# Rescheduling a two-layer bottleneck kernel: first stages further ahead, positions later, filters by halves

## The chip, the cores and the metric

One core of a Trainium2 chip runs the kernel. The engines of a core work side by side, each from its own queue of instructions in order: PE (TensorE: matrix products and transposes), DVE (VectorE), ACT (ScalarE), POOL (GpSimd, which here issues the gathers) and SP (SyncE, which here issues most other transfers). The metric is device time in microseconds (us) for one execution of the whole program; a time quoted as a median is over several executions.

## What is computed

The input x is (4, 1024, 56, 56), float32, and passes through two bottleneck layers.

Layer 0 is a deformable bottleneck. `_conv` is a convolution with bias:

```python
r = jax.nn.relu(_conv(x, w1, b1))                                  # 1x1, 1024 -> 256
r = jax.nn.relu(_deform_conv3x3(r, w2, b2, w_off, b_off))           # 3x3, 256 -> 256
r = _conv(r, w3, b3)                                               # 1x1, 256 -> 1024
x = jax.nn.relu(x + r)
```

In the deformable 3x3 convolution a plain 3x3 convolution of r (256 to 18 channels) gives two offsets for each pixel and each of the nine taps. Each tap reads r at the pixel's place, plus the tap's step, plus its offset, interpolated bilinearly between four neighbours. The nine results are multiplied by the tap's 256 x 256 weights and summed.

Layer 1 is a plain bottleneck with batch normalisation over all four images after each convolution:

```python
out = jax.nn.relu(_bn(_conv(x, w1, b1, 1, 0), g1, be1))             # 1x1, 1024 -> 256
out = jax.nn.relu(_bn(_conv(out, w2, b2, 1, 1), g2, be2))           # 3x3, 256 -> 256
out = _bn(_conv(out, w3, b3, 1, 0), g3, be3)                        # 1x1, 256 -> 1024
x = jax.nn.relu(x + jax.nn.softplus(residual_scale)[0] * out)
```

## The kernel before, in words

**Blocks and stages.** Each image n (four of them) is worked in seven blocks j. Layer 0 passes through these stages; each stage is a Python generator that yields the cost of the matmuls that it has just issued.

- The first stage, `stage_a` (L312 to L427), handles eight rows (448 pixels) of an image. It multiplies x by w1 (matmul L326 over eight chunks of channels, added to a bias that L283 puts into PSUM) and clips the result into `feat` (L318, on ACT). `for_offsets` (L402) multiplies `feat` by the offset weights (`pm`, L407), copies the result (`part`, L416) and stores it in `offc` by small DMAs (L424). `to_table` (L371) transposes `feat` on PE (`ftp`, L380), copies it to the tile `ft` on ACT (L387, L389, L390), and stores it from there in a DRAM table (L394, L398) from which the taps gather. While its own products run, a first stage loads the x of the next block, `following` (`load_x`, L260 to L275, issued on SP). Image 0's seven first stages come ahead of all taps and use a variant of the products with fewer multiplications (class `First`).
- The positions, `stage_b` (L433 to L483): PE transposes a part of `offc` (`po`, L443), ACT copies it (`off`, L458), and about twenty small DVE operations (L459 to L481) turn offsets into gather indices (`idxs`) and bilinear weights (`wts`) for one tap block. In `stage_a(n, j)` the positions of block j - 2 are worked (`if j > 1`), and those of the last two blocks by `last_positions(n)` (L681).
- The taps. The 3136 pixels of an image are cut into tap blocks of 512, 512, 512, 512, 384, 384 and 320 (`SIZES`), and each has nine taps k, 252 in all. `sample` (L489) issues one gather on POOL for each 128 pixels (L495; four neighbours x 256 channels), scales the first neighbour on ACT (L505), and adds the other three on DVE (L507, three instructions). `turn` (L517) transposes the samples on PE (`stp`, L532), copies them on ACT (L538, into `sts`), and forms three sums on DVE (L540 to L542). `tap` (L548) makes the seven products of a Strassen-Winograd step (L560). After tap 8, ACT copies the sums out (L575 to L579), DVE combines them into `r2` (L581 to L587), and ACT clips them (`r`, L589).
- The last stage, `stage_c` (L594 to L667), for one tap block: for each of eight chunks of 128 channels, ACT copies the residual x into PSUM (`pr`, L612), PE adds the product with w3 (L616), ACT clips (`x1t`, L627), and SP stores. The residual is loaded by L605. Then layer 1's 1x1 convolution is done on the same pixels (`acc`, L642), with a copy (L652), statistics (L656) and a store (L657).

**After the taps** layer 1 goes on: a Winograd 3x3 convolution with the transformed filters that `filters` (L685 to L740) made on the way, in the taps of image 3, from loads (L698) and eleven DVE operations on 128 x 1536 elements (L702 to L721), then the statistics, the last 1x1 convolution and the output.

**What sets the order.** The main loop (L944 to L1030) goes through the 252 taps. At tap i it issues the turn of tap i + 1, the samples of tap i + 2 and the products of tap i. Then it adds to a budget the tap's share of all other matmul work (`share`, worked out so that first and last stages come out even over all taps), and steps generators until the budget is spent. `next_stage` (L959) chooses the generator: a first stage of the next image if it is at most one block ahead of the tap block (`first_ones[0][1] <= j + 1`, L961) and in step with the part of the image that has passed, or if no last stage is waiting; otherwise a last stage of a finished tap block from `last_ones`. If there is neither, the loop breaks and the budget stays for later. `due` forces the first stages of the next image to be finished near the image's end. `waiting` holds `last_positions(n)` and is served at once, out of the budget, from the first tap of an image on.

The program order isn't quite the order on the chip: a scheduler under the kernel orders the instructions into the engines' queues, with waits between engines where one needs another's result.

**Buffers.** `gat` has eight gather tiles, `w3p` eight sample tiles `s` and two `sts`, `xin` four tiles for x of first stages, `work` five tiles `r2`, and `worka` one `ft`.

## Time and profile before

| what | value |
|---|---|
| median of three executions | 2836.54 us (2831.96 to 2837.84) |
| the profiled execution | 2833.8 us |
| its span, first to last instruction | 2832.0 us |
| mean granted clock of PE in it | 0.986 |
| matmuls on PE (x12045): busy | 2739.8 us, 97% of the span |
| DVE (x5188): busy | 2175.3 us, 77% |
| ACT (x3045): busy | 1500.8 us, 53% |
| POOL (x1054): busy | 1217.2 us, 43% |
| bytes moved by DMA | 792.70 MB, mean 280 GB/s |
| first tap products, image 0 / 1 / 2 / 3 | 152.5 / 645.7 / 1117.3 / 1597.1 us |
| last tap block's end of products | 2077.3 us |

How to read it: the profile is of one execution. Each engine's busy time is what its instructions took, and since the engines overlap, the shares don't add up to one. An instruction's line (L616) is the line of the kernel that issued it; `pr<-r,w` names what it writes and reads. In a timeline, the number in brackets is how long the engine was idle before the instruction, and what released it. PE can be granted a lower clock after it has been idle; the clock row and the clock columns show that in tenths and as a fraction.

### The profile page before, as it was taken

What the parts mean: (1) busy time and instruction counts of PE and PEld (TensorE: products, weight loads), DVE (VectorE), ACT (ScalarE), POOL (GpSimd) and SP (SyncE); (2) the same over time, 40 slices, a digit from 0 to 9 for tenths busy, and PEclk for the clock granted to TensorE, in tenths of its full rate; (3) what the DMA queues carried; (4) which work ended last, traced back from release to release, by engine and by line L of the source; (5) the groups of instructions that cost most, each with busy time, mean ns of one, the idle gap of its engine ahead of it and who ended that gap; (6) DMA issues with size and microseconds to landing.
All of it is one profiled execution on the core that took longest, in us unless ns stands there. A gap on an engine that the chain in (4) does not pass through costs nothing.

```text
span 2832.0 us, 39691 instructions
## 1 busy us (share of the span) xinstructions
PE 2739.8 (97%) x12045; PEld 1932.4 (68%) x12045; DVE 2175.3 (77%) x5188; ACT 1500.8 (53%) x3045; POOL 1217.2 (43%) x1054
## 2 busy tenths in 40 slices
PE   9979999999999999999999989999989999999999
PEld 7655566677766676667666657666769999874554
DVE  5387777888787889778878888878849987437777
ACT  2245555665655556555564656666652554514444
POOL 0065666576666455656545666554500000111211
PEclk9989999999999999999999999999999999999999
DMA  8598998999999999999998989999930110219998
GB/s 287 180 342 322 327 318 296 362 323 343 342 347 358 337 313 333 338 339 343 359 343 261 349 310 342 350 375 323 314 130 24 48 36 12 93 34 345 352 342 304
DMA packets 313319, 792.70 MB, mean 280 GB/s; under 512 B 33769, under 2 KB 134673, under 8 KB 313105
## 3 DMA queue, kind: packets, MB, share of 16 engines
q0 software_dynamic: 127296, 462.48, 46.0%
q1 hardware_dynamic: 167376, 276.30, 28.4%
q10 hardware_dynamic: 18432, 51.39, 4.6%
q8 instruction: 95, 1.56, 0.2%
q14 instruction: 120, 0.97, 0.1%
HBM read 640.94 MB, written 143.75 MB: 277 GB/s over the span
## 4 chain that ended last, share of the span: by engine, by line
PE 81%; DMA 8%; DVE 6%; ACT 3%; issue 1%; SPq 1%; POOL 0%; ACTq 0%; DVEq 0%; POOLq 0%
PE acc L560 19%; PE acc L642 11%; PE pr L616 10%; PE acc L326 9%; PE q L1192 6%; PE stp L532 6%; DMA g<-table,idxs 5%; PE u L1642 4%; PE c L1642 3%; PE v L1642 3%; PE acc_g L1474 2%; PE pm L407 2%; DVE s L507 2%; PE b L1192 2%; DMA xr<-in_x_dram 1%
## 5 line engine op out<-in xcount | busy, mean ns | idle before, releaser
L495 POOL DMA_INDIRECT g<-table,idxs x900 | 1143.5, 1271 | 908.9 <-DVE s L507 264.2
L507 DVE SCALAR_TENSOR_TENSOR s<-g,wts,s 128x256 f32<-128x256 f32 (+1 forms) x2700 | 1171.9, 478 | 309.7 <-ACT s L505 301.4
L560 PE MATMUL acc<-sts,w 128*128 128x256 f32 (+2 forms) x3528 | 729.0, 356 | 3.7 <-ACT sts L538 2.4
L560 PEld LDWEIGHTS acc<-sts,w 128*128 128x128 f32 x3528 | 604.4, 191 | 54.8 <-ACT sts L538 5.0
L505 ACT ACTIVATE s<-g,wts 128x256 f32<-128x256 f32 x900 | 427.2, 511 | 292.5 <-DMA g<-table,idxs 150.7
L616 PE MATMUL pr<-r,w 128*128 128x512 f32 (+2 forms) x896 | 372.2, 553 | 22.3 <-ACT pr L612 17.1
L642 PE MATMUL acc<-x1t,c1w 128*128 128x512 f32 (+2 forms) x896 | 357.6, 541 | 3.4 <-ACT acc L283 2.2
L532 PEld LDWEIGHTS stp<-ident,s 128*128 128x128 f32 (+1 forms) x1800 | 212.0, 141 | 139.6 <-issue 84.6
L326 PE MATMUL acc<-xt,w 128*128 128x448 f32 x704 | 282.1, 545 | 6.6 <-DMA xt<-in_x_dram 6.6
L616 PEld LDWEIGHTS pr<-r,w 128*128 128x128 f32 x896 | 166.8, 194 | 160.1 <-issue 83.3
L532 PE MATMUL stp<-ident,s 128*128 128x128 f32 (+1 forms) x1800 | 254.8, 274 | 18.1 <-DVE s L507 13.0
L642 PEld LDWEIGHTS acc<-x1t,c1w 128*128 128x128 f32 x896 | 167.9, 190 | 145.1 <-issue 92.6
L538 ACT COPY sts<-stp 128x512 f32<-128x512 f32 (+2 forms) x504 | 242.1, 529 | 19.8 <-PE stp L532 19.7
L627 ACT ACTIVATE x1t<-pr,ch 128x512 f32<-128x512 f32 (+2 forms) x224 | 141.6, 632 | 133.1 <-PE pr L616 130.4
L326 PEld LDWEIGHTS acc<-xt,w 128*128 128x128 f32 x704 | 132.9, 192 | 113.9 <-issue 111.2
L1593 ACT ACTIVATE x1f<-x1f,sh_bn 128x896 f32<-128x896 f32 x112 | 116.0, 1041 | 150.7 <-DVE x1f L1590 125.5
L652 ACT COPY y<-acc 128x512 f32<-128x512 f32 (+2 forms) x112 | 59.2, 529 | 193.2 <-PE acc L642 193.1
L542 DVE TENSOR_TENSOR sts<-sts 128x512 f32<-128x512 f32 (+2 forms) x252 | 155.5, 617 | 0.7
L612 ACT COPY pr<-xr 128x512 f32<-128x512 f32 (+2 forms) x224 | 121.3, 542 | 4.6 <-DMA xr<-in_x_dram 0.3
L1590 DVE SCALAR_TENSOR_TENSOR x1f<-u,sc_bn,x1f 128x448 f32<-128x448 f32 x156 | 106.6, 684 | 18.8 <-PE u L1642 9.4
L1192 PE MATMUL q<-v,u 128*128 128x196 f32 x576 | 108.4, 335 | 8.5 <-DVE v L1144 7.7
L540 DVE TENSOR_TENSOR sts<-sts 128x256 f32<-128x256 f32 (+2 forms) x252 | 97.1, 385 | 24.7 <-ACT sts L538 24.0
(302 smaller groups left out, 3054.0 us busy)
## 6 DMA issues: line engine op xcount, KB each, us to landing
xt<-in_x_dram SPq DMA_DIRECT2D x112, 448.0 KB
x1f<-x_d SPq DMA_DIRECT2D x96, 448.0 KB
out_dram<-x1f ACTq DMA_DIRECT2D x96, 448.0 KB
xr<-in_x_dram SPq DMA_DIRECT2D x128, 256.0 KB
x_d<-x1t SPq DMA_DIRECT2D x128, 256.0 KB
table<-ft SPq DMA_DIRECT2D x56, 384.0 KB
g<-table,idxs POOLq DMA_INDIRECT x900, 7.4
xr<-in_x_dram SPq DMA_DIRECT2D x64, 192.0 KB
```

What stands on the lines that cost most here:

```text
L326: nc.tensor.matmul(acc, w1[:, k, h * 128 : (h + 1) * 128], xts[n, j, k - k % 2][:, k % 2, :], start=start, stop=(k == KC - 1), skip_group_ ...
L495: nc.gpsimd.indirect_dma_start(out=g[:m], out_offset=None, in_=tables[n].rearrange("r q c -> r (q c)"), in_offset=bass.IndirectOffsetOnAxi ...
L505: nc.scalar.activation(s[:m], g[:m, 0:CB], AF.Copy, scale=wt[:, 0])
L507: nc.vector.scalar_tensor_tensor(s[:m], g[:m, corner * CB : (corner + 1) * CB], wt[:, corner], s[:m], ALU.mult, ALU.add,)
L532: nc.tensor.transpose(banks[h][:, t * 128 : t * 128 + m], s[:m, h * 128 : (h + 1) * 128], ident[:m, :m],)
L538: nc.scalar.copy(to, banks[h][:, :size].rearrange("p (e q) -> p e q", e=2))
L542: nc.vector.tensor_sub(sts[:, 5:7, :half], sts[:, 1:4:2, :half], sts[:, 0:2, :half])
L560: nc.tensor.matmul(sums[i], w2[:, a, k], sts[:, b, :half], start=(k == 0 and i % 2 == 0), stop=(k == TAPS - 1), skip_group_check=True,)
L616: nc.tensor.matmul(z, w3[:, h, k * 128 : (k + 1) * 128], r2[:, h, :size], start=False, stop=(h == KB - 1), skip_group_check=True,)
L642: nc.tensor.matmul(z, c1w[:, k, h * 128 : (h + 1) * 128], x1ts[k], start=False, stop=(i == KC // 2 - 1), skip_group_check=True,)
L1192: nc.tensor.matmul(ps[:, o].rearrange("p r c -> p (r c)"), wt, x, start=first and j == 0 and (alone or o == 0), stop=last and j == len(pai ...
L1642: nc.tensor.matmul(to, wt, x, start=start, stop=stop, skip_group_check=True)
```

## The change

Five things are changed together.

- Positions: in images 1 to 3 a first stage works the positions of the block four behind, and no longer two behind (`positions_behind`). `last_positions` therefore has four blocks left, and one step of it is made at each even tap k while any is left, outside the loop that spends the budget. Each step finishes one block's positions (copy and DVE operations) and issues the transposes of the next, so four blocks take five steps, at taps 0, 2, 4, 6 and 8 of tap block 0.
- First stages may run three blocks ahead of the tap block instead of one. With that go two changes of buffers: x of block (1, 2) is loaded by the first stage of (1, 0), and that of (1, 1) loads nothing; and `ft` of block (0, 6) lies in a gather tile instead of `worka`'s only one.
- The clip of a tap block's results (L589) becomes `clip_taps`, called one tap later, just before the block joins `last_ones`.
- The filters' eleven operations are made by halves of 768 columns, and the generator is stepped at eight of nine taps instead of at four.
- `share` leaves out half a block more of last-stage work, which so stays for after the taps (`SIZES[-1] * 3 // 2` instead of `SIZES[-1]`).

```diff
@@ -309,6 +309,11 @@
 
 
 
+        def positions_behind(n):
+
+
+            return 2 if n == 0 else 4
+
         def stage_a(n, j):
 
             b = n * NJ + j
@@ -333,6 +338,9 @@
                 )
 
             following = (n, j + 1) if j + 1 < NJ else (n + 1, 0)
+            if n == 1 and j < 2:
+
+                following = (1, 2) if j == 0 else (N, 0)
             if (n, j) == (0, 0):
 
                 sums = [
@@ -358,18 +366,24 @@
                     for k in range(KC):
                         product(h, k, z, False)
                         if k % 2:
-                            if h == KB - 1 and following != (1, 1):
+                            if h == KB - 1:
                                 load_x(*following, k - 1)
                             yield 2 * BLK
                     clip(h, z, 0.0)
 
                 yield from run([channels(h) for h in range(KB)])
-            if j > 1:
-                yield from stage_b(n, j - 2)
+            behind = positions_behind(n)
+            if j >= behind:
+                yield from stage_b(n, j - behind)
             yield None
 
             def to_table():
-                ft = worka.tile([128, QFULL + 1, CB], F32, tag="ft", name=f"ft_{b}")
+                if (n, j) == (0, NJ - 1):
+
+                    ft = gat.tile([128, 4 * CB], F32, tag="g", name=f"ft_{b}")
+                    ft = ft.rearrange("p (t c) -> p t c", c=CB)
+                else:
+                    ft = worka.tile([128, QFULL + 1, CB], F32, tag="ft", name=f"ft_{b}")
                 for half in range(2):
                     tp = ps1.tile([128, 2, CB], F32, tag="bank", name=f"ftp_{b}_{half}")
                     for i in range(2):
@@ -585,11 +599,17 @@
                 add(r[0][1], r[0][1], p3)
                 add(r[1][0], r[1][1], p4)
                 add(r[1][1], r[1][1], p5)
-                for o in range(KB):
-                    nc.scalar.activation(
-                        r2[:, o, :size], r2[:, o, :size], AF.Relu, bias=col("a_b2", o)
-                    )
                 r2s[n, j] = r2
+
+        def clip_taps(n, j):
+
+            size = SIZES[j]
+            r2 = r2s[n, j]
+            for o in range(KB):
+                nc.scalar.activation(
+                    r2[:, o, :size], r2[:, o, :size], AF.Relu, bias=col("a_b2", o)
+                )
+            last_ones.append((n, j))
 
         def stage_c(n, j):
 
@@ -679,7 +699,7 @@
             nc.scalar.activation(mv[:, 0, 0:1], eps_t, AF.Sqrt)
 
         def last_positions(n):
-            for j in (NJ - 2, NJ - 1):
+            for j in range(NJ - positions_behind(n), NJ):
                 yield from stage_b(n, j)
 
         def filters():
@@ -697,28 +717,37 @@
             for i, t in ((0, w_0), (2, w_2), (1, u3)):
                 nc.sync.dma_start(t.rearrange("p (h j o) -> p h j o", h=KB, j=3), rows[i])
             yield
-            stt = nc.vector.scalar_tensor_tensor
-
-            nc.vector.tensor_add(u1, w_0, w_2)
-            yield
-            nc.vector.tensor_sub(u2, u3, u1)
-            yield
-            nc.vector.tensor_add(u1, u3, u1)
-            yield
-            nc.vector.tensor_scalar_mul(u2, u2, 1.0 / 6)
-            nc.vector.tensor_scalar_mul(u1, u1, -1.0 / 6)
-            yield
-
-            stt(u4, w_2, 4.0, w_0, ALU.mult, ALU.add)
-            yield
-            stt(u3, u3, 2.0, u4, ALU.mult, ALU.add)
-            yield
-            stt(u4, u4, 2.0, u3, ALU.mult, ALU.subtract)
-            yield
-            nc.vector.tensor_scalar_mul(u3, u3, 1.0 / 24)
-            nc.vector.tensor_scalar_mul(u4, u4, 1.0 / 24)
-            yield
-            nc.vector.tensor_scalar_mul(w_0, w_0, 0.25)
+
+            def by_halves(op, *ts):
+                size = each // 2
+                for c in (slice(0, size), slice(size, each)):
+                    op(*(t[:, c] for t in ts))
+                    yield
+
+            def plus(factor):
+                return lambda to, a, b: nc.vector.scalar_tensor_tensor(
+                    to, a, factor, b, ALU.mult, ALU.add
+                )
+
+            def minus(to, a, b):
+                nc.vector.scalar_tensor_tensor(to, a, 2.0, b, ALU.mult, ALU.subtract)
+
+            def times(factor):
+                return lambda t: nc.vector.tensor_scalar_mul(t, t, factor)
+
+
+            yield from by_halves(nc.vector.tensor_add, u1, w_0, w_2)
+            yield from by_halves(nc.vector.tensor_sub, u2, u3, u1)
+            yield from by_halves(nc.vector.tensor_add, u1, u3, u1)
+            yield from by_halves(times(1.0 / 6), u2)
+            yield from by_halves(times(-1.0 / 6), u1)
+
+            yield from by_halves(plus(4.0), u4, w_2, w_0)
+            yield from by_halves(plus(2.0), u3, u3, u4)
+            yield from by_halves(minus, u4, u4, u3)
+            yield from by_halves(times(1.0 / 24), u3)
+            yield from by_halves(times(1.0 / 24), u4)
+            yield from by_halves(times(0.25), w_0)
             nc.sync.dma_start(u0_d, w_0)
             us_0 = w3p.tile([128, 512], F32, tag="x1t", name="us_0", bufs=X1S)
             w_00 = w_0.rearrange("p (h j o) -> p h j o", h=KB, j=3)
@@ -941,11 +970,12 @@
 
 
 
+
         first_ones = [(n, j) for n in range(1, N) for j in range(NJ)]
         last_ones = []
         share = (
             len(first_ones) * (KB * KC * BLK + 3 * BLK + 2 * CB + NT * 128)
-            + (N * HW - SIZES[-1]) * 2 * KB * KC
+            + (N * HW - SIZES[-1] * 3 // 2) * 2 * KB * KC
         ) / (N * HW * TAPS)
 
         running = []
@@ -958,7 +988,7 @@
 
         def next_stage(n, j, passed):
 
-            if first_ones and first_ones[0][0] == n + 1 and first_ones[0][1] <= j + 1:
+            if first_ones and first_ones[0][0] == n + 1 and first_ones[0][1] <= j + 3:
                 if first_ones[0][1] <= passed * (NJ + 1) or not last_ones:
                     running.append(stage_a(*first_ones.pop(0)))
                     return running[-1]
@@ -981,25 +1011,28 @@
                 sample(*nxt)
             tap(n, j, k)
             if done is not None:
-                last_ones.append(done)
+                clip_taps(*done)
             done = (n, j) if k == TAPS - 1 else None
             if (j, k) == (0, 0):
                 waiting = last_positions(n) if n else None
+
+            if waiting and k % 2 == 0:
+                next(waiting, None)
             if (n, j, k) == (N - 1, 1, 0):
                 l0a.close()
                 extra = filters()
-            if extra and k in (1, 3, 5, 7):
+            if extra and k:
                 next(extra, None)
             budget += share * SIZES[j]
             passed = (STARTS[j] + SIZES[j] * k / TAPS) / HW
             while budget > 0 or due(n, j, k):
                 if stage is None:
-                    stage = waiting or upcoming
+                    stage = upcoming
                     if stage is None:
                         stage = next_stage(n, j, passed)
                         if stage is None:
                             break
-                    elif stage is upcoming:
+                    else:
                         upcoming = None
                 cost = next(stage, 0)
                 if cost == LAST:
@@ -1007,15 +1040,13 @@
                     if upcoming is not None:
                         next(upcoming)
                 elif cost == 0:
-                    if stage is waiting:
-                        waiting = None
                     stage = None
                 elif cost in (None, BEGUN):
                     if not due(n, j, k):
                         break
                 else:
                     budget -= cost
-        last_ones.append(done)
+        clip_taps(*done)
         while last_ones or stage or upcoming:
             if stage is None:
                 if upcoming is None and len(last_ones) == 1:
```

## Prediction

> **What bounds the kernel now.** I read the page first, then the table of windows by stage, then PE's waits, then the timelines around PE's longest gaps. All quoted durations are from the one profiled execution of before: 2833.8 us, of which the span is 2832.0.
>
> Page, parts 1 and 2 (busy share; then tenths in 40 slices of 70.8 us):
>
> ```profile
> PE 2739.8 (97%) x12045; PEld 1932.4 (68%) x12045; DVE 2175.3 (77%) x5188; ACT 1500.8 (53%) x3045; POOL 1217.2 (43%) x1054
> ...
> PE   9979999999999999999999989999989999999999
> ...
> PEclk9989999999999999999999999999999999999999
> ```
>
> PE is busy 97%. It is the bound nearly everywhere, so only its idle time (92 us in all) and its half-clock time can be won. The lowest digits, PE's 7 and the clock's 8, sit in slice 3 (142 to 212 us), the start of image 0's taps; the 8 in slice 24 (1628 to 1699 us) is the start of image 3's.
>
> The table of windows puts numbers on that: image 0's first 36 taps (152 to 412 us), the rest of image 0, image 1 to its last blocks, image 2, image 3.
>
> ```profile
> core 0: us, PE busy (x) PEld busy (x) DVE busy (x) ACT busy (x) POOL busy (x), PEclk, DMA share, GB/s
> 152.00:412.00 260.00, 233.31 (x937) 149.28 (x936) 206.19 (x527) 139.68 (x288) 164.50 (x119) 0.95 0.91 323
> 412.00:667.00 255.00, 252.88 (x1160) 176.93 (x1159) 202.62 (x547) 150.86 (x335) 159.08 (x123) 1.00 0.96 330
> 667.00:1108.00 441.00, 437.91 (x1942) 299.91 (x1941) 358.88 (x958) 253.14 (x548) 259.78 (x210) 1.00 0.95 339
> ...
> 1590.00:2078.00 488.00, 475.04 (x2008) 328.73 (x2007) 397.38 (x976) 304.90 (x649) 269.88 (x215) 0.99 0.92 325
> ```
>
> First stretch: 260 - 233.3 = 26.7 us idle, and a clock of 0.95, worth 0.05 x 233.3 = 11.7 us of work: 38.4 us lost. The next stretch loses 2.1 us. So image 0's beginning loses 36.3 us more than a normal stretch of its length.
>
> PE's waits name the releasers, all small groups:
>
> ```profile
> PE pr L616 <- ACT pr L612: 17.1, 7, 4.8
> PE stp L532 <- DVE s L507: 13.0, 11, 4.7
> PE q L1192 <- DVE v L1144: 7.7, 2, 7.5
> PE pm L407 <- ACT sts L538: 7.3, 3, 4.0
> ```
>
> The mechanism of a typical gap, in the timelines of POOL, DVE, ACT and PE (start, length, what, idle before):
>
> ```profile
> 404.87 6.42 POOL L495 DMA_INDIRECT g<-table,idxs  x1 [0.30 <-ACT s L505]
> ```
> ```profile
> 403.28 7.21 DVE L507 SCALAR_TENSOR_TENSOR s<-g,wts,s 128x256 f32<-128x256 f32 x18
> ```
> ```profile
> 406.02 0.51 ACT L505 ACTIVATE s<-g,wts 128x256 f32<-128x256 f32 x1 [1.50 <-DMA g<-table,idxs]
> 406.44 0.67 ACT L627 ACTIVATE x1t<-pr,ch 128x512 f32<-128x512 f32 x1
> 407.14 0.59 ACT L612 COPY pr<-xr 128x512 f32<-128x512 f32 x1
> ```
> ```profile
> 407.78 5.83 PE L616 MATMUL pr<-r,w 128*128 128x512 f32 x9 [3.70 <-ACT pr L612]
> ```
>
> In image 0 a first stage may run only one block ahead (L961), so for whole blocks there is nothing to put beside the taps; the budget piles up and then pays out one last stage as a burst of about 20 us, in which PE is busy and DVE and ACT starve. After it DVE runs flat out, a gather (normally 0.94 to 1.3 us on POOL) takes 6.42, ACT's in-order queue stands at L505 waiting for a gather, and the residual's copy into PSUM (L612), which PE's next product adds to, stands behind it. PE idles 3.70 us and then runs 3.4 us at half clock.
>
> The other cluster is the filters in image 3:
>
> ```profile
> 1639.29 1.76 DVE L702 TENSOR_TENSOR u<-ends 128x1536 f32<-128x1536 f32 x1 [7.73 <-issue]
> 1640.97 0.48 DVE L507 SCALAR_TENSOR_TENSOR s<-g,wts,s 128x256 f32<-128x256 f32 x1
> 1641.36 1.75 DVE L712 SCALAR_TENSOR_TENSOR u<-ends 128x1536 f32<-128x1536 f32 x1
> ```
>
> L702 waits for loads issued at 1621 to 1627 and holds DVE 7.73 us, then two operations of 1.75 us stand within three of the taps' own. PE pays with gaps of 4.67 us (before 1643.57) and 4.82 us (before 1684.00).
>
> **What the Trainium skill says.** "TensorE: Matmul & The Clock Gate", Part 1, What's actually happening: after an idle window of about 3.4 us TensorE falls to half clock and needs a busy window to return. The trace agrees: its half-clock spells are 3.4 or 6.8 us long and follow the gaps above. So a gap costs its length and about half of a spell: 3.7 + 1.7 here. "SBUF — State Buffer", the "DVE blocks DMA" trap: a DMA issued from GpSimd's queue needs descriptors, which can't be written while DVE holds the ports they share. The page ties this to DVE's faster modes; the trace shows the same stretch under L507, the gather ending 0.81 us after the unbroken DVE run. "DMA: Bandwidth & Descriptors", Where 436 GB/s comes from: about 358 GB/s is HBM's side for a core. The windows show 323 to 339 at a DMA share of 0.91 to 0.96, so there is little room for packing more traffic into a stretch.
>
> **The change part by part.** No matmul is added or removed; the built order has the same ones, and POOL's order is the same. So every gain is idle or half-clock time of PE.
>
> First stages up to three blocks ahead. In the built order the stages of blocks 9 and 10 move up into taps (0,0,5) to (0,1,3), and the largest piece of other matmuls between two taps falls from about 22 to about 11 us (counted in the built orders at 0.90 us for a 512-column product, as L616's eight rows take 3.60). Each moved stage carries four loads of 448 KB on SP and its table and offset stores with it; they pass only last-stage loads of blocks that haven't begun. What is recovered: of the 36.3 us, the gaps of the very first taps (155 to 183 us, 9.6 us by PE's timeline) and their two spells (3.4 and 6.8 us, worth 5.1) belong to filling the pipeline and stay: 14.7. The rest is 21.6; I take 20, because some gathers will still be stretched. Bounds: 8 (rival A) and 36 (all of it). What is late next: the gathers, since DVE needs 12 x 0.40 + 2 x 0.335 + 0.60 = 6.07 us for a 512-pixel tap (L507 from 7.21 / 18 above, L540 to L542 by their distances on DVE's timeline), and a tap must last 7.2 us or more to cover that.
>
> Filters by halves, later. Before, the cluster costs 4.67 + 4.82 of gaps and two spells of 6.8 us (6.8 lost): 16.3 us. The last load was issued at 1626.99 and DVE reached the wait at 1631.56. In the built order of after the work between the two is longer by 1.5 to 4.5 us, so a wait of 3 to 6 us instead of 7.73 remains; halves are 1.75 / 2 = 0.88 us, one per step, so at most one stands before a tap's operations. DVE pays 11 more instructions, well under 1 us, beside PE's work. The first wait's 4.67 us gap shrinks or goes, the second goes with the long operations: I take 9 of 16.3. Bounds 0 and 16.
>
> Positions four blocks behind. In images 1 to 3 four of them instead of two come in the taps of block 0, each about 2.5 us of small DVE operations (L459 to L481) behind one ACT copy L458. So + 2 x 2.5 = 5 us of DVE in a block of 77.8 us (image 1; 645.7 to 723.5 by its first tap matmuls), where DVE needs 9 x 6.07 + 2.6 + 5 = 62 us: 67 of 77.8 fits. The same work leaves the blocks before. Queued behind an L459 that waits are the next tap's L507 operations, and behind those stp L532 on PE. Cost zero while DVE has its 10 us of slack; without that cover it is rival B. Bounds -4 (the two stalls, 4.04 us before 1156.41 and its like, go) and +12 (two more of 5.7). I take 0.
>
> Tap results clipped a tap later: two ACT operations of 0.67 us (L589) leave the place behind seven DVE additions, where PE's waits on L589 are 5.0 us in two cases; 4.03 of that is at the very end of the taps, where nothing moves. At most 1 us; I take 0. Half a block of last stages kept for the end: from the taps (3,6,0) on, PE's order is the same in both, and the 4.03 and 7.54 us gaps before 2081.58 and 2109.31 stay: 0. Loads of (1,2) early and ft of (0,6) in another buffer: the opening's table stores go some 4 us sooner, but the offsets' copy stays behind a clip on ACT, and PE's gap of 4.27 us before 143.70 with it: 0.5, between 0 and 2.
>
> Sum: 20 + 9 + 0 + 0 + 0.5 = 29.5. 2833.8 - 29.5 = 2804.3. The profiled execution lies 2.7 us below the median of the runs (2836.54), so 2807.0.
>
> **The rivals.** A, the gaps only move: with image 0's stretch shortened by 20 us its traffic would run at 323 x 260 / 240 = 350 GB/s, above every stretch here. If 343 (the best sustained slices) is the limit, the cap is 260 x (1 - 323/343) = 15 us, and if half of the gathers' stalls come back elsewhere, 8; with 4 from the filters, whose loads are still waited for, 12: 2824. For it: DMA share of 0.91 already. Against: page slices of 362 and 375.
>
> B, slower: four positions on even taps make DVE's runs unbroken at the start of each image, and each such run stretches a gather, as at 1141.00 (6.34 us) ahead of the gap of 4.04 us before 1156.41; a stall costs 4.04 + 1.7 = 5.7. There are 12 such places. At more than 29.5 / 5.7 = 5 of them the change loses; at 8, 46 - 29.5 = 16 slower: 2853. Against: one tap in two only, and 10 us of slack per block. For: DVE has 86% of that block then.
>
> C, nearly everything goes: 36 + 14 + 2 = 52, thus 2785. Against: the pipeline's filling needs its gathers.
>
> D, the change doesn't do what it says: lookahead is offered but the order on the queues makes up for it, or losses of B cancel gains: about 2836.
>
> **How the numbers follow.** Forecast 0.50 (own range 2795 to 2821, from 8 less to 12 more with the bounds taken together), A 0.20, B 0.16, C 0.07, D 0.07. About 0.2% (5.7 us) is what a measurement of this kernel tells from no change. Faster by over that: 0.50 + 0.20 + 0.07 = 0.77; within 0.07; slower 0.16. The range 2790 to 2842 leaves out most of B and of C's lower half.
>
> **What would show it.** Right: the first 240 us of taps have under 12 us of idle PE and a clock of 0.97 or more; no gap above 3 us behind L612 there; the wait of the first filter operation is under 6 us, and no PE gap above 2 us beside it; the opening's and the end's gaps are as before. Wrong: POOL gathers of 6 us at taps (1,0), (2,0), (3,0) with PE gaps behind them (B); the windows' idle time of image 0 unchanged, or the same sum found in 412 to 667 (A).

## The result, and the profile after

The changed kernel takes 2803.22 us (median of six executions, 2791.22 to 2813.96) against 2837.19 us for the kernel before (six executions, 2831.96 to 2840.76). The ratio is 0.9885, with a 95% interval of 0.9856 to 0.9914: about 1.15% faster, 34 us. The forecast was 2807.0 us. The profiled execution of the changed kernel took 2791.22 us (span 2789.4 us), the lowest of the six, so a comparison of the two profiles shows 42.6 us where the medians show 34. This difference has a place, which is shown below.

In the changed kernel the line numbers have moved: the residual's copy L612 is L632, the product with w3 L616 is L636, `acc` L642 is L662, and the gathers L495 and samples L505 and L507 are L509, L519 and L521.

The windows of the changed kernel, cut at the first tap products of blocks (0,0), (0,1), (0,4) and (1,0). PEclk is the mean granted clock, and the DMA share is the mean busy share of the core's 16 DMA engines:

```profile
core 0: us, PE busy (x) PEld busy (x) DVE busy (x) ACT busy (x) POOL busy (x), PEclk, DMA share, GB/s
149.50:217.20 67.70, 61.10 (x275) 40.59 (x275) 63.77 (x167) 36.04 (x79) 47.88 (x39) 0.95 0.94 334
217.20:444.80 227.60, 227.17 (x924) 148.82 (x923) 187.93 (x460) 137.03 (x281) 127.52 (x113) 1.00 0.99 366
444.80:609.80 165.00, 163.76 (x802) 118.33 (x801) 136.26 (x375) 101.81 (x233) 90.05 (x80) 1.00 0.97 333
```

The same cuts in the kernel before:

```profile
152.50:218.40 65.90, 52.94 (x244) 35.81 (x244) 57.92 (x150) 32.37 (x70) 46.18 (x36) 0.90 0.93 335
218.40:473.90 255.50, 241.77 (x938) 154.06 (x937) 190.23 (x482) 139.63 (x286) 154.19 (x113) 0.97 0.91 320
473.90:645.70 171.80, 170.56 (x830) 121.26 (x829) 141.98 (x398) 104.71 (x240) 107.16 (x82) 1.00 0.97 334
```

Read the middle rows first: blocks (0,1) to (0,3). Before, PE idles 255.5 - 241.8 = 13.7 us there and loses 0.03 x 241.8 = 7.3 us to the clock: 21.0. After, it idles 0.4 us at full clock. The matmuls are nearly as many (924 rows against 938). The first rows, block (0,0), tell another story: 18.3 us lost before (13.0 idle and 0.10 x 52.9), 9.7 after, in this execution.

PE's waits and the filters in the changed kernel:

```profile
PE q L1223 <- DVE v L1175: 7.7, 2, 7.5
PE acc L662 <- ACT acc L283: 7.3, 3, 4.0
PE pr L636 <- ACT pr L632: 6.9, 4, 4.3
```
```profile
1621.05 0.78 SPq L718 DMA_DIRECT2D u<-in_b_w_dram  x1
```
```profile
1634.60 0.96 DVE L724 TENSOR_TENSOR u<-ends 128x768 f32<-128x768 f32 x1 [8.35 <-DMA y_d<-y]
```
```profile
1644.11 5.83 PE L662 MATMUL acc<-x1t,c1w 128*128 128x384 f32 x12 [4.04 <-ACT acc L283]
1677.69 5.10 PE L636 MATMUL pr<-r,w 128*128 128x384 f32 x8 [4.28 <-ACT pr L632]
```

The waits behind the residual's copy fell from 17.1 us to 6.9, and none of these is left in image 0's first four blocks. But the first filter operation (now L724) still waits, 8.35 us, and PE still has two gaps above 4 us beside the filters.

Where the time went, by tap block (from each block's first tap product to the next's; microseconds; one execution each). "After, again" is a second profiled execution of the changed kernel.

| blocks | before | after | after, again | filters held |
|---|---|---|---|---|
| start to (0,0) | 152.5 | 149.5 | 151.0 | 151.4 |
| (0,0) | 65.9 | 67.8 | 79.2 | 73.3 |
| (0,1) to (0,3) | 255.5 | 227.6 | 228.8 | 226.8 |
| (0,4) to (0,6) | 171.8 | 165.0 | 164.9 | 163.7 |
| image 1 | 471.6 | 470.7 | 472.3 | 470.4 |
| image 2 | 479.8 | 477.2 | 479.4 | 478.1 |
| (3,0) and (3,1) | 169.2 | 168.3 | 166.7 | 158.3 |
| (3,2) to the end of the taps | 311.0 | 309.9 | 309.9 | 309.9 |
| after the taps | 754.7 | 753.5 | 755.8 | 753.5 |

Two things stand out. Blocks (0,1) to (0,3) gain 26 to 29 us, and do so in all six profiled executions with the changed order there (226.8 to 229.6 us). Block (0,0) varies from execution to execution by 11 us with the same order of instructions; in the profiled execution of the changed kernel it was short.

### The profile page after: what moved, and what is told of

Same layout as the page of the kernel before. It is cut to its first block, busy times and chain, and to the rows that moved or that the text cites. A ratio compares the mean times of both kernels' runs of the same rounds, so it can differ in the third digit from the quotient of the medians.

```text
span 2789.4 us, 39697 instructions
## 1 busy us (share of the span) xinstructions
PE 2722.1 (98%) x12045; PEld 1927.4 (69%) x12045; DVE 2183.5 (78%) x5199; ACT 1496.3 (54%) x3045; POOL 1169.8 (42%) x1054
## 4 chain that ended last, share of the span: by engine, by line
PE 85%; DVE 6%; DMA 5%; ACT 2%; issue 1%; SPq 1%; ACTq 0%; POOL 0%; DVEq 0%
PE acc L574 21%; PE acc L662 12%; PE pr L636 11%; PE acc L331 8%; PE q L1223 7%; PE stp L546 6%; PE u L1673 3%; DVE s L521 3%; PE acc_g L1505 2%; PE c L1673 2%; PE v L1673 2%; PE pm L421 2%; PE b L1223 2%; DMA g<-table,idxs 2%; PE acc L867 1%
## 5 line engine op out<-in xcount | busy, mean ns | idle before, releaser
L509 POOL DMA_INDIRECT g<-table,idxs x900 | 1096.4, 1218 | 914.8 <-DVE s L521 228.9
L521 DVE SCALAR_TENSOR_TENSOR s<-g,wts,s 128x256 f32<-128x256 f32 (+1 forms) x2700 | 1173.8, 477 | 258.0 <-ACT s L519 125.4
L519 ACT ACTIVATE s<-g,wts 128x256 f32<-128x256 f32 x900 | 425.6, 511 | 215.2 <-PE stp L546 85.3
L636 PE MATMUL pr<-r,w 128*128 128x512 f32 (+2 forms) x896 | 366.7, 546 | 11.0 <-ACT pr L632 6.9
L662 PE MATMUL acc<-x1t,c1w 128*128 128x512 f32 (+2 forms) x896 | 360.8, 545 | 9.1 <-ACT acc L283 7.3
L662 PEld LDWEIGHTS acc<-x1t,c1w 128*128 128x128 f32 x896 | 168.4, 191 | 149.8 <-issue 100.0
L636 PEld LDWEIGHTS pr<-r,w 128*128 128x128 f32 x896 | 166.0, 192 | 143.6 <-issue 86.8
L546 PE MATMUL stp<-ident,s 128*128 128x128 f32 (+1 forms) x1800 | 248.8, 273 | 3.9 <-DVE s L521 3.1
L632 ACT COPY pr<-xr 128x512 f32<-128x512 f32 (+2 forms) x224 | 121.5, 542 | 3.8
```

What stands on the lines that cost most here:

```text
L509: nc.gpsimd.indirect_dma_start(out=g[:m], out_offset=None, in_=tables[n].rearrange("r q c -> r (q c)"), in_offset=bass.IndirectOffsetOnAxi ...
L519: nc.scalar.activation(s[:m], g[:m, 0:CB], AF.Copy, scale=wt[:, 0])
L521: nc.vector.scalar_tensor_tensor(s[:m], g[:m, corner * CB : (corner + 1) * CB], wt[:, corner], s[:m], ALU.mult, ALU.add,)
L546: nc.tensor.transpose(banks[h][:, t * 128 : t * 128 + m], s[:m, h * 128 : (h + 1) * 128], ident[:m, :m],)
L636: nc.tensor.matmul(z, w3[:, h, k * 128 : (k + 1) * 128], r2[:, h, :size], start=False, stop=(h == KB - 1), skip_group_check=True,)
L662: nc.tensor.matmul(z, c1w[:, k, h * 128 : (h + 1) * 128], x1ts[k], start=False, stop=(i == KC // 2 - 1), skip_group_check=True,)
```

## The experiments

All ratios are to the kernel before on the same chip, with 95% intervals. The first question was which of the five parts gains anything, then why it does, then what became of the filters.

**Positions and lookahead alone.** The changed kernel with the other three parts undone:

```diff
-            if extra and k:
+            if extra and k in (1, 3, 5, 7):
-            + (N * HW - SIZES[-1] * 3 // 2) * 2 * KB * KC
+            + (N * HW - SIZES[-1]) * 2 * KB * KC
```
with the filters' operations whole and L589's clip in `tap` again.

> Positions four behind and first stages three ahead (with their two changes of buffers) alone; filters, clip and share as before. Theory: this pair is what the change gains, by taking away image 0's gaps: ratio to before 0.988 to 0.991, image 0's taps (first products of (0,0) to first products of (1,0)) in about 460 us against 493. Rival: the gain is spread over the five parts, so this pair has at most two thirds of it: ratio 0.992 or more.

Measured: ratio 0.9903 (0.9888 to 0.9918), 2810.38 us. Blocks (0,1) to (0,3) take 229.1 us, image 0's taps 468.6. So the pair gains 0.97% of the changed kernel's 1.15%; what is left for the other three parts is within the measurement's width.

**Lookahead of one and of two blocks.** In the changed kernel:

```diff
-            if first_ones and first_ones[0][0] == n + 1 and first_ones[0][1] <= j + 3:
+            if first_ones and first_ones[0][0] == n + 1 and first_ones[0][1] <= j + 1:
```

> The changed kernel with first stages one block ahead again; all else stays changed. Theory: image 0's idle time returns (about 27 us idle and a clock of 0.95 between the first product of taps and 412 us), and with it some 30 us: ratio to before 0.997 to 1.001. Rival (positions four behind and the clip a tap later relieve the queues by themselves): at least half of the gain stays, ratio 0.994 or less.

Measured: 0.9999 (0.9987 to 1.0011). The whole gain is gone, with positions, clip, filters and share all still changed. Blocks (0,1) to (0,3) take 259.0 us, and the gaps behind the residual's copy are back in the same three places (3.71, 3.77 and 3.44 us, before the products of taps (0,1,2), (0,2,2) and (0,3,2)).

And with `j + 2`:

> The changed kernel with first stages at most two blocks ahead. Theory (the gain goes with how much of image 0's start has first-stage work to put beside the taps): about half of the lookahead's gain, ratio to before 0.993 to 0.996. Rival (two blocks suffice, the third is never used): as the changed kernel, 0.988 to 0.991.

Measured: 0.9916 (0.9890 to 0.9942), which lies between the two expected bands, so about 70% of the gain; blocks (0,1) to (0,3) take 240.4 us, between 227.6 and 259.0. The third block is used, for some 13 us in those blocks.

**Bursts halved in the kernel before.** The lookahead gives PE work where it had none, and it takes the bursts away. To part the two, the kernel before was given a limit on what it can save up:

```diff
-            budget += share * SIZES[j]
+            budget = min(budget, share * SIZES[j]) + share * SIZES[j]
```

> The kernel before with its unspent budget limited to one tap's share, and nothing else: first stages stay one block ahead, so the idle taps at the start get no other work, but the last stages of image 0 no longer come in bursts (largest piece between two taps halved), and some 13 us of them stay for after the taps. Theory as predicted (the bursts cause the stalls by starving DVE and then driving it flat out): the gaps behind the copy of the residual in image 0 (3.27, 2.85, 3.70 us) go, 8 to 15 us gained: ratio 0.995 to 0.997. Rival (what the change gives is work for PE where it had none; the bursts are only how that shows): the gaps may go, but the time doesn't: ratio 0.999 to 1.002.

Measured: 1.0022 (1.0011 to 1.0034), slower, as the rival said or a little worse. The gaps before taps (0,2,2) and (0,3,2) went, but the first one, before (0,1,2), didn't (PE, then the gather on POOL that ran ahead of it):

```profile
248.25 2.08 PE L616 MATMUL pr<-r,w 128*128 128x512 f32 x2 [6.49 <-ACT pr L612]
```
```profile
233.63 7.15 POOL L495 DMA_INDIRECT g<-table,idxs  x1 [0.30 <-ACT s L505]
```

Blocks (0,1) to (0,3) took 244.7 us, 10.8 less than before, with some 3 us less other work in them. The first tap block still had taps with nothing beside them, as before, and then a piece of 11 us. Elsewhere the kernel lost: images 1 and 2 took 480.6 and 489.9 us (471.6 and 479.8 before), and what came after the taps, with some 11 us more matmul work in it, took 5.6 us longer. So it doesn't part the two causes: empty and full taps still alternate, only less. A better test keeps the sum of the work in each place.

**The same work, bunched, in the changed kernel.** In image 0's blocks 1 to 3 the stages are stepped only at every m-th tap:

```diff
-            while budget > 0 or due(n, j, k):
+            while (budget > 0 or due(n, j, k)) and not (n == 0 and 0 < j < 4 and k % 2):
```

(`k % 4` in the second kernel). With m = 2 each block has exactly the same other matmuls as in the changed kernel; with m = 4 the three blocks have them together.

> The changed kernel, in which the first and last stages are stepped only at every second tap in image 0's blocks 1 to 3; each of these blocks has the same other matmuls in sum as in the changed kernel, but taps with none alternate with taps with 9 to 19 us of them. Theory (taps with no other work let DVE run flat out behind, stretch the gathers, and make PE wait behind the copy of the residual): stalls return, 5 to 20 us in these three blocks together (227.6 us in the changed kernel). Rival (only the sum of the work in a block counts): these three blocks keep their length within 3 us.

> The same with steps only at taps 0, 4 and 8 of image 0's blocks 1 to 3: three taps of four have no other matmuls, the fourth up to 18 us of them (33 at one place), with the same sum over the three blocks. Theory: more than with every second tap, 20 to 45 us in these three blocks, most of the lookahead's gain lost: ratio to before 0.996 to 1.004. Rival: the three blocks stay within 3 us of the changed kernel's 227.6 us, ratio 0.986 to 0.991.

Measured: with every second tap 0.9967 (0.9952 to 0.9982), and the three blocks take 253.1 us against 227.6 (25.5 longer); with every fourth 1.0053 (1.0035 to 1.0072), and they take 279.7 us (52 longer). Both are more than expected. With every second tap nearly the whole 28 us of these blocks' gain is gone, though not a matmul was moved out of them. So it is the place of the work within them, and not only its sum, that the lookahead buys.

Block by block, with every second tap:

```profile
231.40:320.80 89.40, 79.81 (x325) 49.81 (x323) 65.09 (x161) 48.98 (x101) 56.26 (x41) 0.98 0.94 335
320.80:396.30 75.50, 75.50 (x296) 49.43 (x295) 55.94 (x136) 44.61 (x89) 45.01 (x35) 1.00 0.91 324
396.30:484.50 88.20, 78.58 (x308) 49.29 (x307) 62.51 (x162) 46.67 (x94) 53.81 (x38) 0.98 0.86 307
```

The changed kernel's three blocks took 77.3, 75.4 and 74.9 us, so the middle block lost nothing. There the taps really alternate, 3.9 us with no other work and 12.5 to 13.3 us with it, and PE has no idle time. The other two lost 12.1 and 13.3 us. In them the work came out in larger pieces: two or three taps of 4 to 7 us in a row, then one of 22 to 26 us, and those three long taps hold 11.0 of the 19.2 us of idle time. A single short tap between two long ones was free here; runs of short taps weren't.

The three blocks together, with every second tap:

```profile
231.40:484.50 253.10, 233.89 (x924) 148.53 (x923) 183.55 (x457) 140.25 (x282) 155.08 (x113) 0.99 0.91 322
```

and with every fourth:

```profile
230.60:510.30 279.70, 245.42 (x925) 152.20 (x924) 183.68 (x456) 140.88 (x282) 152.51 (x113) 0.94 0.84 297
```

The DMA share falls from 0.99 to 0.91 and 0.84, although the bytes are nearly the same. The timelines of POOL, DVE, ACT and PE in one such spell show why:

```profile
372.74 1.07 POOL L509 DMA_INDIRECT g<-table,idxs  x1 [11.57 <-DVE sts L556]
```
```profile
369.98 0.48 DVE L521 SCALAR_TENSOR_TENSOR s<-g,wts,s 128x256 f32<-128x256 f32 x1 [13.35 <-ACT s L519]
```
```profile
383.75 0.51 ACT L519 ACTIVATE s<-g,wts 128x256 f32<-128x256 f32 x1 [4.71 <-DMA g<-table,idxs]
386.44 0.51 ACT L519 ACTIVATE s<-g,wts 128x256 f32<-128x256 f32 x1 [2.18 <-DMA g<-table,idxs]
389.14 0.51 ACT L519 ACTIVATE s<-g,wts 128x256 f32<-128x256 f32 x1 [2.19 <-DMA g<-table,idxs]
```
```profile
395.95 2.07 PE L636 MATMUL pr<-r,w 128*128 128x512 f32 x2 [7.26 <-ACT pr L632]
```

While PE works off the burst (until 369), DVE stands 13.35 us and POOL 11.57 us: the eight gather tiles (four for a tap) are taken, two taps ahead, and no gather starts. Then come three taps with 4 us of PE work each, which eat up the two taps in store; ACT waits for gather after gather at L519, in its queue's order, and the residual's copy stands behind it. PE idles 7.26 us. In blocks 1 to 3 of this kernel no gather instruction took 5 us or more, so one stretched to 6 us isn't needed for the stall. But two gathers of this spell took 2.28 and 2.47 us instead of about 1, and what they add isn't separated; nor did a run change the number of gather tiles.

**The filters, whole again.** In the changed kernel only the filters are as before.

> The changed kernel with the filters' operations whole and stepped at four taps of nine, as before. The prediction's step (the filters gain 9 us): ratio to before 0.9915 to 0.9925. Rival, from the trace of the changed kernel, where the first filter operation still waits 8.35 us and PE still has gaps of 4.04 and 4.28 us beside the filters: the part is worth under 3 us, ratio 0.988 to 0.990.

Measured: 0.9904 (0.9888 to 0.9920), which is in neither of the two expected bands. The trace places it: blocks (3,0) and (3,1) take 164.0 us together, less than the 168.3 and 166.7 with halves, while block (0,0), whose order is the same in both, took 81.0 us in the profiled execution against 67.8 and 79.2. So the higher median can't be put down to the filters; in the blocks where they work, whole operations lost nothing against halves. Their first operation waited there too, for less time:

```profile
1648.46 1.76 DVE L723 TENSOR_TENSOR u<-ends 128x1536 f32<-128x1536 f32 x1 [4.10 <-DMA ends<-in_b_w_dram]
```

**The filters held back.** The program steps the first operation a tap or two after the loads, but on DVE's queue it came up about 5 us after the last load's issue in both kernels (4.6 before, 5.2 after). The scheduler seems to place it by its own estimate of when the loads land, which no run tested. Here each operation is queued behind the sums of the tap at which it is stepped (an order on DVE's queue alone, no wait between engines):

```diff
-                    op(*(t[:, c] for t in ts))
+                    with tc.issue_after(turns[0].ins):
+                        op(*(t[:, c] for t in ts))
```
```diff
-            nc.vector.tensor_sub(sts[:, 5:7, :half], sts[:, 1:4:2, :half], sts[:, 0:2, :half])
+            turns[0] = nc.vector.tensor_sub(
+                sts[:, 5:7, :half], sts[:, 1:4:2, :half], sts[:, 0:2, :half]
+            )
```

> The changed kernel with each half operation of the filters queued on DVE behind the three sums of the tap in whose turn it is stepped, so that one comes per tap, and the first about two taps later than in the changed kernel. Theory (the wait for the filters' loads is what costs, as it stands ahead of the taps' own operations): no wait above 2 us before the first filter operation, PE's gaps of 4.04 and 4.28 us and their half-clock spells of 3.4 and 6.8 us go, 8 to 13 us less than the changed kernel: ratio to before 0.984 to 0.986. Rival (DVE has too little slack there, so that any filter operation costs PE its length): same as the changed kernel within 3 us, with the gaps elsewhere in image 3.

Measured: 0.9862 (0.9841 to 0.9883), 2795.33 us. Blocks (3,0) and (3,1) take 158.3 us, 10 less than in the changed kernel; no PE gap above 0.9 us lies beside the filters. On DVE's timeline the first operation comes at 1665.29 with no wait:

```profile
1665.29 0.95 DVE L728 TENSOR_TENSOR u<-ends 128x768 f32<-128x768 f32 x1
1673.56 0.95 DVE L728 TENSOR_TENSOR u<-ends 128x768 f32<-128x768 f32 x1
```

The same edit, halves included, on the kernel before:

> The kernel before with the filters' operations by halves, each queued on DVE behind the sums of the tap at which it is stepped; nothing else. Theory (the filters' loss is the wait for their loads at the head of DVE's queue, apart from the rest): the blocks (3,0) and (3,1), 169.2 us before, take 157 to 162, ratio 0.996 to 0.998. Rival (image 3's first blocks lose their time to the positions and last stages that fall there): they keep 166 us or more.

Measured: 0.9944 (0.9926 to 0.9962), a larger gain than expected. Blocks (3,0) and (3,1) take 154.3 us instead of 169.2, so 14.9 us of the cluster's 16.3 can be had without anything else of the change. The window of the two blocks in the kernel before:

```profile
1597.10:1766.30 169.20, 157.51 (x628) 107.55 (x627) 147.92 (x354) 101.89 (x213) 107.52 (x76) 0.96 0.94 336
```

and with the operations held back:

```profile
1609.50:1763.80 154.30, 152.62 (x628) 104.87 (x627) 135.52 (x340) 99.42 (x211) 87.79 (x74) 1.00 0.98 357
```

The same 628 matmul rows; the idle time falls from 11.7 to 1.7 us and the clock is whole.

And held back, but whole, in the changed kernel:

> The kernel with held filter operations, but each operation whole (1536 columns), one at eight taps of nine. Theory (what costs is the wait for the loads at the head of DVE's queue, not the length of an operation): blocks (3,0) and (3,1) in 157 to 161 us, as with halves (158.3), ratio to before 0.985 to 0.988. Rival (a whole operation of about 1.75 us ahead of a tap's own is what stalls PE): 163 us or more, with PE gaps over 1.5 us beside the operations.

Measured: 0.9873 (0.9854 to 0.9892). The two blocks take 157.6 us, as with halves. One gap of 2.78 us appeared in block (3,2), which took 79.2 us against 74.7, in the one execution that was profiled. So the wait decides, and not the length of an operation, as far as one execution of each tells.

**Positions spread.** In images 1 and 2 the last four positions at taps 0, 5, 10, 15 and 20, in the kernel with held filters:

```diff
-            if waiting and k % 2 == 0:
+            if waiting and (k % 2 if n == N - 1 else (TAPS * j + k) % 5) == 0:
```

> The kernel with held filter operations, and in images 1 and 2 the last four positions stepped at every fifth tap (0, 5, 10, 15, 20) instead of at the even taps of the first block. Theory (four positions in nine taps overfill DVE there: the first blocks of images 1 and 2 take 79.8 and 85.0 us in the changed kernel, 77.8 and 81.7 before): these two blocks shorten by 2 to 4 us each: ratio to before 0.983 to 0.986. Rival (the two blocks are longer because more first-stage and last-stage work falls in them): they keep their length within 1 us, and the time is that of the kernel with held operations.

Measured: 0.9863 (0.9840 to 0.9887), no different from the kernel with held filters (0.9862). Block (2,0) shortened to 79.9 us from 85.6, but (1,1) grew to 81.0 from 76.5, with a wait of 2.18 us behind a position's copy L472 before tap (1,1,6), and (1,0) stayed at 80.1, in one execution each. A position seems to cost a few microseconds now and then where it falls, and moving it moves the cost.

**The changed kernel again**, beside these:

> The changed kernel once more, unaltered, beside the others of this call. Theory: what differs between its executions is the first tap block (67.8 us here, 73.3 and 81.0 us in two kernels with the same order of instructions there), so the runs spread over about 2790 to 2815 us again: ratio to before 0.986 to 0.991. Rival: the blocks of image 3 with the filters differ as much.

Measured: 0.9883 (0.9861 to 0.9904), 2800.63 to 2809.86 us. In the profiled executions of kernels whose image 0 is the same, block (0,0) took 67.8, 79.2, 81.0, 73.3, 78.4 and 69.2 us, while (0,1) to (0,3) took 226.8 to 229.6 in all of them.

## Why the prediction was right, step by step

The time was right (2807.0 forecast, 2803.22 measured), and the largest step was in its main point. Two terms of the sum were mis-sized, in opposite directions, and that they nearly cancel is luck. A slip in the working: the range's upper end, 2821, stands for 14 us less gain than forecast, and not for the 8 named beside it.

Of the signs named, the first 240 us of taps had 7.0 us of idle PE at a clock of 0.99 in the profiled execution, as said, but 17.2 us in the repeated one, more than the 12 allowed. No gap above 3 us is left there behind the residual's copy. The signs at the filters failed.

**First stages up to three blocks ahead: 20 us forecast.** The main point held: with a lookahead of one the gain is gone, and bunching the work again brings stalls back. The working said that of 36.3 us lost some 14.7 belong to the first taps and stay, and 21.6 goes. In blocks (0,1) to (0,3) the loss fell from 21.0 to 0.4 us, so 20.6 went. The first part stayed, too, on the whole: block (0,0) lost 18.3 us before, 9.7 in the lucky execution and 19.2 in the repeated one (79.2 - 63.8 idle and 0.06 x 63.8). What the working left out is that work also moves forward into block (0,0) (275 matmul rows against 244, some 10 us of work) and fills part of its idle time. Image 0's taps as a whole took 493.2 and 504.1 us in two kernels that have before's order there, and 460.3 to 473.6 in six executions with the changed one: roughly 30 us, half as much again as forecast. PE's idle time and clock loss in them, added up from its instructions and clock records, came to 40 and 50 us, and to 12 to 25. About 2 us of the 30 are matmuls that moved out of image 0's taps, and two executions of before's order are few to set the rest by.

**The chain of causes was right in its ends, but its middle had the order wrong.** The prediction went from a burst to DVE running flat out, to a stretched gather and so to the stall. In blocks (0,1) to (0,3) of the kernel before, no stall follows a burst. The bursts fall in taps (0,1,1), (0,2,1) and (0,3,1), which last 32, 29 and 24 us; the taps behind them last 7.3 to 9.0 us, with no idle PE. Each gap lies inside a burst, 7 to 13 us after its tap's first product, and ahead of the burst stand two or three short taps (4.8 and 6.0 us; 6.5, 5.3 and 3.2; 3.8, 6.5 and 5.9). With a lookahead of one and of two blocks the gaps lie in the same way. So the taps left without work bring the stall, and the burst is where it shows: DVE needs 6.07 us for a 512-pixel tap by the prediction's own estimate, and a run of shorter taps uses up the store of two. This is read from the traces; the middle block with every second tap agrees, and no run varied it alone.

Gathers did get quicker: those over 2.2 us in image 0's taps fell from 28 to 8 (12 in the repeated execution), and 16 to 20 in each of the other images stayed. With the work bunched they came back, 23 and 24, so a share of the stalls may be theirs. "SBUF — State Buffer", its "DVE blocks DMA" trap, may describe what lengthens a single gather, and no run here tests it by itself.

Half clock follows idle time, as "TensorE: Matmul & The Clock Gate", Part 1, What's actually happening, has it: 0.94 with work at every fourth tap, 0.99 with every second (where no gap is over 2.9 us), 1.00 without gaps. But the page's idle window of about 3.4 us wasn't needed: in the kernel before, spells of 3.4 us followed single gaps of 2.12 and 2.85 us (before 110.56 and 322.61), while one of 2.23 us (before 892.05) had none. There the measurement decides. One spell there lasted 10.2 us, longer than the prediction said.

**Filters by halves, later: 9 us forecast, and the step that failed.** The size of the cluster was right (16.3 us estimated, 14.9 gained by holding the operations back in the kernel before). But the changed kernel gets next to nothing of it: 169.2 us before, 168.3 and 166.7 after, and 168.0 to 170.4 in the four kernels with one or two blocks of lookahead or bunched work, which have the same filters and the same matmuls there. These two blocks have some 2 us more matmul work than before (640 rows against 628), so idle time and clock loss did fall, by 1 to 4 us; but halves can't be the reason, since whole operations did no worse (164.0). The term that failed is "a wait of 3 to 6 us instead of 7.73 remains": it was 8.35. Both the loads and the first operation moved later in image 3, and in time the distance hardly grew: DVE reached the wait 5.2 us after the last load's issue (1621.05 to 1626.25), as against 4.6 before, and was released 13.5 us after it, as against 12.3. The second half of the step, that shorter operations take the second gap away, failed too: 4.28 us against 4.82, and whole operations held back do as well.

**Positions four behind: 0 forecast.** Right in the sum. The first blocks of images 1 and 2 took 79.8 and 85.0 us instead of 77.8 and 81.7, which would be a trace of rival B, at 2 to 3 us each and not 5.7 per position; but with before's order and held filters they took 81.5 and 81.2, so it isn't clear of what executions vary. The images as wholes took 470.7 and 477.2 instead of 471.6 and 479.8.

**The clip a tap later, and half a block kept for the end: 0 forecast.** The kernel with all but the changed filters and the kernel with positions and lookahead alone differ by just these two, and measure 0.9904 and 0.9903. The end's gaps are where they were (4.02 and 7.52 us against 4.03 and 7.54).

**The opening: 0.5 forecast.** PE's gap ahead of the first positions is 3.97 us instead of 4.27 (3.6 to 4.2 in the other executions). The first taps begin at 149.5 to 152.4 us in kernels with the changed opening and at 151.7 to 152.5 in those with that of before: about 1 us on the mean.

Rival A's cap didn't hold: blocks (0,1) to (0,3) ran at 366 GB/s (355 to 366 in the six executions with the changed order there), above the 343 that it took for the limit. "DMA: Bandwidth & Descriptors", Where 436 GB/s comes from, gives about 358 for a core; the trace shows that much or slightly more over these 228 us, and the measurement decides. At a DMA share of 0.99 the stretch has little left to give.

In sum: about 30 from image 0 instead of 20, next to nothing from the filters instead of 9, and 1 at the opening, against 34 by the medians, where block (0,0) alone varies by 11. The total was closer than its terms.

The kernel with held filters has the lowest ratio found, 0.9862; beside 0.9885 and 0.9883 for the changed kernel the intervals overlap, so that it beats the changed kernel as a whole rests on the two blocks: 158.3 us (157.6 with whole operations, 154.7 with positions spread) against 168.3 and 166.7. Against the kernel before it is clear.

## What to carry to other kernels

Where several engines pass work along a chain with a small store between them (two taps of gathers here), it isn't enough that each stretch has the right sum of other work. One step without fill was free here; two or three in a row used up the store and stalled the chain. A scheduler's lookahead should be long enough that it always has a piece to offer. An operation that needs a transfer belongs in the queue where the transfer has landed by the clock, not by a count of steps; look for the first instruction of a new kind and at its wait, and tie its place to something in the queue. And when one block varies by 10 us between executions of the same program, compare the other blocks, not the totals.

## What the runs showed of the hardware that was not expected

The three filter loads (2.4 MB together) cleared DVE's wait only 12.3 and 13.5 us after the last was issued, with the DMA engines busy all that time (a share of 1.03 and 1.01 in these two stretches, where a packet counts whole if it starts there). The releaser that the profile infers in the changed kernel is a store of y issued between them (1617.26), and whether that store or the loads came last wasn't separated.

The transfers of blocks (0,1) to (0,3) held 355 to 366 GB/s over 227 to 230 us, once PE took its work without gaps. Spells of half clock came after single gaps of 2.12 and 2.85 us. Of the 83 gathers over 2.2 us in the kernel before, 47 ended 0.8 us after an unbroken run of DVE instructions, which is a coincidence in time and was not tested.
